# A two-layer convolution block: a new order of its second layer, and 64 channels expanded two phases at a time

## The chip, the cores and the metric

The kernel runs on one core of a Trainium2 chip. The core has a matrix engine (TensorE, PE in the profile; its weight loads are PEld), a vector engine (VectorE, DVE), an activation engine (ScalarE, ACT), GpSimd (POOL) and SyncE (SP), which here only issues DMAs. The metric is the device time of one execution in microseconds (us). The kernel before takes 4761.99 us, the median of three runs (4741.11 to 4764.95).

## The reference

Thirty-two images of 96 channels and 56 x 56 points pass through two layers. Cut to what matters:

```python
x = x + L0(group_norm(x))          # layer 0
x = x + L1(group_norm(x))          # layer 1

def L0(x):                         # inverted bottleneck, 4-bit weights and activations
    h = act_q(bn1(conv1x1(x, w1)))         # 96 -> 576 channels ("expand")
    h = act_q(bn2(depthwise3x3(h, w2)))    # 576 channels
    return x + bn3(conv1x1(h, w3))         # 576 -> 96 ("project")

def L1(x):                         # three groups of 32 channels
    x_0, x_05, x_1 = split(x)
    x_0  = conv3x3(x_0, conv0_w * gate(mean(x_0)))             # "spatial"
    F    = frft2d(x_05, alpha(mean(x_05)))                     # fractional Fourier transform
    F    = conv1x1(F, conv05_w * gate(mean(x_05)))             # "fractional mix"
    x_05 = abs(frft2d(F, -alpha)) / (H * W)                    # a square root at its end
    x_1  = irfft2(conv1x1(rfft2(x_1), conv1_w * gate(mean(x_1))))
    return conv3x3(concat(x_0, x_05, x_1), conv2_w)            # "final"
```

The group norms are over 32 groups of three channels, per image. The gates and `alpha` are small networks of the channel means.

## The kernel before

The program is a software pipeline over the images. While layer 0 of image i+1 is on its way, layer 1 of image i fills in. Both are given as lists of steps with weights, and `interleave` mixes two lists; a scheduler then fixes the order of every engine's instructions when the program is built. Each engine works through its own list in that order.

```python
    def layer0(i):
        xt = xts[i]
        def norm():                                     # statistics of the loaded image
            stats = p2.tile([C, NCH, 6], F32, tag="bn", name=f"bn{i}")
            for j in range(NCH):
                nc.vector.bn_stats(stats[:, j, :], xt[:, j * CN : (j + 1) * CN])
            mean, rstd, _ = group_stats(...)
        # ... split(k): DVE makes v, ACT rounds it to vh, DVE takes the rest vl; per quarter
        #     ("phase") of the image
        def expand(b, k):                               # block b of 128 channels, phase k
            ps = pair(f"pe{i}_{b}_{k}")
            for n, v in enumerate((s["vh"], s["vl"])):
                for h in range(2):
                    nc.tensor.matmul(ps[:, h, :HN], w1[:, 128 * b : 128 * (b + 1)],
                        v[:, k, HN * h : HN * (h + 1)], start=(n == 0), stop=(n == 1))
            src = q1s[turn["q1s"] % 3]
            quant_act(ps, A1[:, b : b + 1], B1[:, b : b + 1], src[:, :, :PH], ...)   # ACT to qt, DVE to q1s
            for g in range(blk(b) // G):                # four (last block: two) DMAs q1s -> qp
                nc.sync.dma_start(out=qps[(NB * i + b) % 3][...], in_=src[...])
        # ... depthwise(b, j): 8 matmuls into a pair `pd`, quant_act to qtd and q2
        # ... project(h, lo, hi): 72 matmuls into two pairs `pp`, then DVE adds them to x
```

PSUM is used as two pairs of banks (`pair`: pe, pd and pp share them) and four single banks (`bank`: all of layer 1). The image tiles `x` have three buffers, so the load of image i+2 goes to the buffer that image i-1 was stored from. `qt` has three buffers.

```python
        def mix_f(j):                                   # before: 4 steps, each both halves
            at = slice(HN * j, HN * (j + 1))
            for h in range(2):
                t = p2.tile([128, HN], F32, tag="zs", ...)
                nc.tensor.matmul(ps[:, :HN], g1[rows], s["xf"][rows, at], start=True, stop=True)
                # half 1 to zs on DVE, half 0 on ACT
                nc.sync.dma_start(out=s["z"][:, h, at], in_=t)          # to DRAM
            if j < 3: return
            # ... two DMAs z -> zh (the other way round in memory), eight DMAs z -> az
        # rows_f(g): matmuls pi of zh, copied to Y;  columns_f(g): matmuls pz of Y, plus az,
        # squared on ACT (sq), added on DVE (Z)
        def magnitude():
            for r in range(4):
                nc.scalar.activation(dst[:, :, r, :], s["Z"][G * r : G * (r + 1)], AF.Sqrt)   # to cat
        # spatial(h): ps -> cat;  hilbert(g): pr -> cat
        def final(j):                                   # rows 8j .. 8j+7 of the output
            for t in range(9):
                nc.tensor.matmul(ps[:C, :CN], wc[:, C * t : C * (t + 1)], cat[...], ...)      # pc
            nc.vector.scalar_tensor_tensor(part, ps[:C, :CN], bc, part, ALU.add, ALU.add)

        first = [(0.5, means), (1.0, gates), (0.1, norm)]
        steps = [(0.5, weights), (1.0, angles)] + each(1.1, mix_t, 4) + each(1.0, mix_f, 4)
        sp = each(2.7, spatial, 2)
        steps += sp[:1] + each(2.1, hilbert, 2) + each(1.3, rows_f, 4) + each(1.2, columns_f, 4)
        steps += [(0.0, magnitude)] + sp[1:]
        steps += each(6.7, final, NCH)
        return first, steps, [(0.0, store)]

    for i in range(B):
        conv, nxt = now["conv"], None
        if i + 1 < B:
            nxt = layer0(i + 1)
            conv[8:8] = nxt["norm"]
            at = 2 * (4 * NB - LEAD) + 1
            conv[at:at] = nxt["split"]
        interleave(conv, one[:-4])
        interleave(now["last"], one[-4:-2])             # project
        head, two, done = layer1(i)
        interleave(head + (nxt["first"] if nxt else []), one[-2:] + end)
        if i + 2 < B:
            load(i + 2)
        one, end, now = two, done, nxt
```

So layer 1 of an image gets five of its seven final convolutions under layer 0 of the next one, and two are held for the time in which the gates of the image after it are worked out.

Of the kernel before, what the change touches and what calls it, by code (L numbers as in the profile page):

```python
# [37 lines left out]
F32 = mybir.dt.float32  # L38
F32R = mybir.dt.float32r
# [3 lines left out]
AF = mybir.ActivationFunctionType  # L43
# [4 lines left out]
C, H, W = 96, 56, 56  # L48
HW = H * W
HID = 576  # L50
NB = 5
# [3 lines left out]
G = 32  # L55
NG0 = HID // G
PH = H // 2
PN = PH * PH
PW = PH + 2
PT = (PH + 1) * PW + 2  # L60
HN = PN // 2
HH = HW // 2
LOW = 64
LEAD = 7
L = 57
MAGIC = 1.5 * 2.0**23
TWO_PI = 6.283185
# [10 lines left out]
def blk(b):  # L78
    return 128 if b < NB - 1 else HID - 128 * (NB - 1)
# [7 lines left out]
def interleave(a, b):  # L87

    ta, tb = sum(c for c, _ in a) or 1, sum(c for c, _ in b) or 1
    i = j = 0  # L90
    ca = cb = 0.0
    while i < len(a) or j < len(b):
        if j >= len(b) or (i < len(a) and ca * tb <= cb * ta):
            ca += a[i][0]
            a[i][1]()
            i += 1
        else:
            cb += b[j][0]
            b[j][1]()
            j += 1  # L100
# [3 lines left out]
def block_kernel(ctx: ExitStack, tc: tile.TileContext, out: bass.AP, a: dict):  # L104
    nc = tc.nc
# [3 lines left out]
    cp = ctx.enter_context(tc.tile_pool(name="const", bufs=1))  # L109
    xp = ctx.enter_context(tc.tile_pool(name="xp", bufs=3))  # L110
    p1 = ctx.enter_context(tc.tile_pool(name="p1", bufs=1))
    p2 = ctx.enter_context(tc.tile_pool(name="p2", bufs=2))
    p3 = ctx.enter_context(tc.tile_pool(name="p3", bufs=3))
    dp = ctx.enter_context(tc.tile_pool(name="dp", bufs=2, space=bass.MemoryType.DRAM))
    ps0 = ctx.enter_context(tc.tile_pool(name="ps0", bufs=2, space=PSUM))
    ps1 = ctx.enter_context(tc.tile_pool(name="ps1", bufs=4, space=PSUM))

    def bank(pool, name):
        return pool.tile([128, 512], F32, tag="bank", name=name)

    def pair(name):

        return ps0.tile([128, 2, 512], F32, tag="pair", name=name)
# [19 lines left out]
    def prepare():  # L143
# [29 lines left out]

        w1f = load_tmp("w1")
        quantise(w1f, C, HID, "1")
        w1 = cp.tile([C, NB * 128], F32R, tag="w1r", name="w1r")
        nc.vector.memset(w1f[:, HID:], 0.0)
        nc.vector.tensor_copy(w1, w1f)
        w2 = load_tmp("w2")
        quantise(w2, 128, NG0 * 16, "2")  # L180
        mask = load_tmp("mask")
# [55 lines left out]
    w1, dw, w3, A1, B1, A2, B2, A3, B3, cw = prepare()  # L237
# [12 lines left out]


    q1s, qps = [], []
    for k in range(3):
        t = cp.tile([128, PH, PW], FP8, tag=f"q1s{k}", name=f"q1s{k}")
        nc.gpsimd.memset(t, 0.0)
        q1s.append(t)
    for k in range(3):
        t = cp.tile([128, 4, PT], FP8, tag=f"qp{k}", name=f"qp{k}")
# [10 lines left out]
    for k in range(2):  # L269
        t = cp.tile([G + 1, 1], F32, tag=f"hid{k}", name=f"hid{k}")  # L270
# [4 lines left out]
    g1 = cp.tile([128, 128], F32, tag="g1", name="g1")  # L275
# [9 lines left out]
    zh = cp.tile([LOW + W, G, LOW], F32, tag="zh", name="zh")  # L285
# [32 lines left out]
    turn = {"q1s": 0}  # L318
# [6 lines left out]
    def layer0(i):  # L325

        xt = xts[i]
        s = {}
# [37 lines left out]
            nc.vector.tensor_scalar(xt, xt, s["one"], s["off"], ALU.mult, ALU.add)  # L366

        def expand(b, k):
            ps = pair(f"pe{i}_{b}_{k}")
            for n, v in enumerate((s["vh"], s["vl"])):  # L370
                for h in range(2):
                    nc.tensor.matmul(  # L372
                        ps[:, h, :HN],
                        w1[:, 128 * b : 128 * (b + 1)],
                        v[:, k, HN * h : HN * (h + 1)],
                        start=(n == 0),
                        stop=(n == 1),
                    )
            src = q1s[turn["q1s"] % 3]
            turn["q1s"] += 1  # L380
            quant_act(ps, A1[:, b : b + 1], B1[:, b : b + 1], src[:, :, :PH], f"e{i}_{b}_{k}")

            n, at = blk(b) // G, PW * (k // 2) + k % 2
            for g in range(n):
                nc.sync.dma_start(  # L385
                    out=qps[(NB * i + b) % 3][G * k : G * (k + 1), g, at : at + PH * PW],
                    in_=src[g * G : (g + 1) * G].rearrange("c h w -> c (h w)"),
                )

        def depthwise(b, j):  # L390
            g = 4 * b + j
# [38 lines left out]
                nc.vector.bn_stats(stats2[i][:, j, :], xt[:, j * CN : (j + 1) * CN])  # L430


        ex = [(0.75, lambda b=b, k=k: expand(b, k)) for b in range(NB) for k in range(4)]
        de = [(1.45, lambda g=g: depthwise(g // 4, g % 4)) for g in range(NG0)]
        conv = []
        for g in range(NG0):
# [13 lines left out]
    def layer1(i):  # L450
        xt = xts[i]
        s = {}
# [191 lines left out]
        def mix_f(j):  # L644

            if j == 0:
                s["z"] = dp.tile([128, 2, HH], F32, tag="z", name=f"z{i}")
            at = slice(HN * j, HN * (j + 1))
            for h in range(2):
                t = p2.tile([128, HN], F32, tag="zs", name=f"zs{i}_{j}_{h}")  # L650
                rows = slice(LOW * h, LOW * h + G + 2)
                ps = bank(ps1, f"pm{i}_{j}_{h}")
                nc.tensor.matmul(ps[:, :HN], g1[rows], s["xf"][rows, at], start=True, stop=True)  # L653
                if h:
                    nc.vector.tensor_copy(t, ps[:, :HN])
                else:
                    nc.scalar.copy(t, ps[:, :HN])
                nc.sync.dma_start(out=s["z"][:, h, at], in_=t)
            if j < 3:
                return  # L660
            z = s["z"].rearrange("o u n -> o (u n)")
            for k in range(2):
                nc.sync.dma_start(
                    out=zh[LOW * k : LOW * k + W, :, :W], in_=z[G * k : G * (k + 1)].rearrange("o (h w) -> h o w", w=W)
                )
            az = p1.tile([128, H // 4, 2, W], F32, tag="az", name=f"az{i}")
            s["az"] = az
            for r in range(4):
                for t in range(2):
                    src = z[2 * G + G * t : 3 * G + G * t].rearrange("o (q r w) -> r o q w", r=4, w=W)  # L670
                    nc.sync.dma_start(out=az[G * r : G * (r + 1), :, t, :], in_=src[r])

        def rows_f(g):
# [20 lines left out]
        def columns_f(g):  # L694

            if g == 0:
                s["Z"] = p1.tile([128, H // 4, W], F32, tag="Z", name=f"Z{i}")
            n = 4 if g < 3 else 2
            ps = bank(ps1, f"pz{i}_{g}")
            for k in range(n):  # L700
                q = 4 * (4 * g + k)
                nc.tensor.matmul(
                    ps[:, 2 * W * k : 2 * W * (k + 1)],
                    Y[:, q : q + 4, :].rearrange("p h c -> p (h c)"),
                    cs,
                    start=True,
                    stop=True,
                )
            m = 2 * W * n
            sq = p2.tile([128, 8 * W], F32, tag="zs", name=f"sq{i}_{g}")  # L710
            add = s["az"][:, 4 * g : 4 * g + n].rearrange("p q t w -> p (q t w)")
            nc.vector.tensor_tensor(sq[:, :m], ps[:, :m], add, ALU.add)
            nc.scalar.activation(sq[:, :m], sq[:, :m], AF.Square)
            z = sq[:, :m].rearrange("p (q r w) -> p q r w", r=2, w=W)
            nc.vector.tensor_tensor(s["Z"][:, 4 * g : 4 * g + n, :], z[:, :, 0, :], z[:, :, 1, :], ALU.add)

        def magnitude():
            dst = cat[G : 2 * G, 1 : 1 + H, 1 : 1 + W].rearrange("p (q r) w -> p q r w", r=4)
            for r in range(4):
                nc.scalar.activation(dst[:, :, r, :], s["Z"][G * r : G * (r + 1)], AF.Sqrt)  # L720

        def spatial(h):

# [35 lines left out]
        def each(c, f, n):  # L759
            return [(c, lambda k=k: f(k)) for k in range(n)]  # L760

        first = [(0.5, means), (1.0, gates), (0.1, norm)]
        steps = [(0.5, weights), (1.0, angles)] + each(1.1, mix_t, 4) + each(1.0, mix_f, 4)
        sp = each(2.7, spatial, 2)
        steps += sp[:1] + each(2.1, hilbert, 2) + each(1.3, rows_f, 4) + each(1.2, columns_f, 4)
        steps += [(0.0, magnitude)] + sp[1:]
        steps += each(6.7, final, NCH)
        return first, steps, [(0.0, store)]

# [1 line left out]
    now = layer0(0)  # L771
# [3 lines left out]
    one, end = [], []  # L775
    for i in range(B):
        conv, nxt = now["conv"], None
        if i + 1 < B:
            nxt = layer0(i + 1)
            conv[8:8] = nxt["norm"]  # L780
            at = 2 * (4 * NB - LEAD) + 1
            conv[at:at] = nxt["split"]


        interleave(conv, one[:-4])
        interleave(now["last"], one[-4:-2])
        head, two, done = layer1(i)
        interleave(head + (nxt["first"] if nxt else []), one[-2:] + end)
        if i + 2 < B:
            load(i + 2)  # L790
        one, end, now = two, done, nxt
# [86 lines left out]
def _layout(inputs):  # L878
# [3 lines left out]
    f = np.float32  # L882
    k = _constants()
# [2 lines left out]

    def hidden(v):

        p = np.zeros((NB * 128,) + v.shape[1:], f)
        p[:HID] = v  # L890
        return np.moveaxis(p.reshape((NB, 128) + v.shape[1:]), 0, 1)

    k["x"] = np.asarray(inputs["x"])
# [79 lines left out]
```

## Time and profile before

| | before |
|---|---|
| time, median of 3 runs | 4761.99 us |
| profiled span | 4750.5 us |
| TensorE matmul busy | 4293.0 us, 90% |
| VectorE busy | 2393.3 us, 50% |
| ScalarE busy | 2177.6 us, 46% |
| DMA moved | 249.58 MB, 53 GB/s on average |
| longest matmul groups | pc (final) 1620.7, pd (depthwise) 956.8, pe (expand) 434.7 + 351.7 |

How to read the lines that follow. A group is written as output <- inputs by tile name, so `pm<-xf,g` is the matmul of the fractional mix and `zs<-pm` its copy out of PSUM. A line of waits names who waited, for whom, how long in total, how often and the longest. In the timeline each line has its start, its length, the engine, the line of the kernel, the operation, and in brackets how long the engine was idle before it and what ended that. A line of windows has the stretch, its length, and each engine's busy time (and number of instructions) in the order PE, PEld, DVE, ACT, POOL, then the granted share of TensorE's clock, the share of DMA time and GB/s. A wait that ends with several semaphores is put down to one of them.

Tile names: `bn` statistics of a loaded image, `x` image tile, `vv` and `xf` inputs of the fractional mix, `pm` its product, `z`, `zh`, `az` its way through DRAM, `pi` and `pz` the two transform steps, `cat` the input of the final convolution, `pc` its output, `pp` the projection, `pj`, `pvv`, `px`, `po`, `pmb` smaller matmuls of layer 1.

### The profile page before, as it was taken

The numbers are of one execution on the slowest core, as the hardware profiler recorded it, in microseconds if no ns is written. First come the engines' busy times: TensorE is split into PE (matmuls) and PEld (weight loads), VectorE is DVE, ScalarE is ACT, GpSimd is POOL, SyncE is SP. The second block draws the span as 40 slices with busy tenths as digits, with TensorE's granted clock in tenths as the row PEclk, the third lists the DMA queues.
The fourth block names the chain that finished last, engine by engine and source line by source line (L and its number), as shares of the span: only waits on it lengthen the run. The fifth ranks groups of instructions, "written<-read, shape, count | busy, mean of one in ns | idle before, by whom it ended". The sixth has DMA issues, their size and how long they took to land.

```text
span 4750.5 us, 59888 instructions
## 1 busy us (share of the span) xinstructions
PE 4293.0 (90%) x21632; PEld 2471.1 (52%) x21632; DVE 2393.3 (50%) x5385; ACT 2177.6 (46%) x2824; POOL 176.7 (4%) x209
## 2 busy tenths in 40 slices
PE   3799999999998999999999999999999999999987
PEld 2545555545555555555555555455555555555544
DVE  5545545545445455455454455454454554555532
ACT  3534445444455444455444454444454444554431
POOL 1000000000000000000000000000000000000000
PEclk9899999999999999999999999999999999999998
DMA  2212222211223211222211222122222112222112
GB/s 72 44 48 45 42 61 65 64 46 39 48 62 65 62 38 36 59 64 65 58 40 39 58 65 64 43 42 48 62 65 63 35 39 58 65 64 53 33 34 48
DMA packets 397243, 249.58 MB, mean 53 GB/s; under 512 B 283233, under 2 KB 390100, under 8 KB 390804
## 3 DMA queue, kind: packets, MB, share of 16 engines
q1 hardware_dynamic: 394368, 242.76, 23.0%
q8 instruction: 172, 2.82, 0.3%
q10 hardware_dynamic: 2580, 2.99, 0.2%
q14 instruction: 123, 1.01, 0.1%
HBM read 92.90 MB, written 89.92 MB: 38 GB/s over the span
## 4 chain that ended last, share of the span: by engine, by line
PE 63%; DVE 14%; DMA 11%; ACT 6%; issue 4%; SPq 3%; POOL 0%; DVEq 0%; ACTq 0%; POOLq 0%
PE pc L746 31%; PE pd L398 12%; PE pp L414 5%; DMA zh<-z 4%; PE pe L372 4%; PE pm L653 4%; DMA qp<-q1s 3%; PE pi L678 3%; ACT cat L720 2%; SPq L385 2%; DMA z<-zs 2%; DVE bn L333 2%; DVE q1s L315 2%; DVE x L426 2%; DMA x<-in_x_dram 1%
## 5 line engine op out<-in xcount | busy, mean ns | idle before, releaser
L746 PE MATMUL pc<-cat,wc 96*96 96x448 f32 x4032 | 1620.7, 557 | 60.9 <-ACT cat L720 60.9
L746 PEld LDWEIGHTS pc<-cat,wc 96*96 96x96 f32 x4032 | 664.1, 168 | 895.5 <-issue 809.0
L398 PE MATMUL pd<-qp,dw 128*128 128x392 fp8e4 x4608 | 956.8, 353 | 43.0 <-ACT qtd L313 37.9
L313 ACT ACTIVATE qtd<-pd,o,s 128x784 int16<-128x784 f32 x576 | 576.4, 1001 | 908.1 <-PE pd L398 878.2
L313 ACT ACTIVATE qte<-pe,o,s 128x784 int16<-128x784 f32 x640 | 635.9, 998 | 685.3 <-PE pe L372 669.5
L398 PEld LDWEIGHTS <-dw 128*128 128x128 fp8e4 x4608 | 447.4, 102 | 502.2 <-issue 203.9
L372 PE MATMUL pe<-vh,w1r 96*128 96x392 f32 x1280 | 434.7, 422 | 71.1 <-DVE x L426 41.2
L315 DVE TENSOR_SCALAR q1s<-qte 128x784 fp8e4<-128x784 int16 x640 | 358.8, 562 | 240.4 <-ACT qte L313 144.3
L315 DVE TENSOR_SCALAR q<-qtd 128x784 bf16<-128x784 int16 x576 | 207.0, 359 | 499.1 <-ACT qtd L313 496.4
L754 DVE SCALAR_TENSOR_TENSOR x<-pc,bc,x 96x448 f32<-96x448 f32 x224 | 152.0, 679 | 582.7 <-PE pc L746 581.2
L372 PE MATMUL pe<-vl,w1r 96*128 96x392 f32 x1280 | 351.7, 357 | 0.0
L372 PEld LDWEIGHTS pe<-vh,w1r 96*128 96x128 f32 x1280 | 221.8, 198 | 222.2 <-issue 94.9
L653 PE MATMUL pm<-xf,g 34*128 34x392 f32 x512 | 202.7, 768 | 107.5 <-DVE bn L333 105.0
L414 PE MATMUL pp<-q,w3q 32*96 32x392 bf16 x4608 | 255.8, 327 | 2.2 <-DVE x L426 2.2
L372 PEld LDWEIGHTS pe<-vl,w1r 96*128 96x128 f32 x1280 | 246.1, 198 | 0.5
L426 DVE SCALAR_TENSOR_TENSOR x<-pp,s,x 96x392 f32<-96x392 f32 x256 | 142.2, 616 | 175.8 <-PE pp L414 175.8
L414 PEld LDWEIGHTS <-w3q 32*96 32x96 bf16 x4608 | 182.0, 118 | 84.6 <-issue 31.5
L726 PE MATMUL ps<-xq,g 128*128 128x392 f32 x512 | 201.1, 536 | 0.0
L678 PE MATMUL pi<-cs,zh 120*120 120x112 f32 x1024 | 136.9, 295 | 63.8 <-DMA zh<-z 57.9
L333 DVE BATCH_NORM_STATS2 bn<-x 96x6 f32<-96x448 f32 x224 | 121.1, 608 | 133.6 <-DMA x<-in_x_dram 133.6
L361 ACT CAST vh<-v 96x392 fp32r<-96x392 f32 x256 | 126.2, 516 | 128.7 <-DVE v L353 127.9
L678 PEld LDWEIGHTS pi<-cs,zh 120*120 120x120 f32 x1024 | 131.6, 209 | 75.6 <-DVE cat L640 24.1
(149 smaller groups left out, 3881.5 us busy)
## 6 DMA issues: line engine op xcount, KB each, us to landing
qp<-q1s SPq DMA_DIRECT2D x2304, 26.2 KB
z<-zs SPq DMA_DIRECT2D x256, 196.0 KB
x<-in_x_dram SPq DMA_DIRECT2D x32, 1176.0 KB
out_dram<-x SPq DMA_DIRECT2D x32, 1176.0 KB
zh<-z SPq DMA_DIRECT2D x64, 392.0 KB
az<-z SPq DMA_DIRECT2D x256, 98.0 KB
xf<-vv SPq DMA_DIRECT2D x128, 6.1 KB
prep<-in_w_dram ACTq DMA_DIRECT2D x1, 864.0 KB
```

The costliest lines, as they stand in the source:

```text
L313: nc.scalar.activation(t.rearrange("p (h n) -> p h n", h=2), ps[:, :, :HN], AF.Relu, bias=offset, scale=scale)
L315: nc.vector.tensor_scalar(dst, src, 15.0, None, ALU.min, saturate=False if dst.dtype == FP8 else None)
L333: nc.vector.bn_stats(stats[:, j, :], xt[:, j * CN : (j + 1) * CN])
L372: nc.tensor.matmul(ps[:, h, :HN], w1[:, 128 * b : 128 * (b + 1)], v[:, k, HN * h : HN * (h + 1)], start=(n == 0), stop=(n == 1),)
L398: nc.tensor.matmul(ps[:, h, :HN], dw[:, g, t, :], view(qps[(NB * i + b) % 3][:, j, :], at, [[PW, PH // 2], [1, PH]]), start=(t == 0), stop ...
L414: nc.tensor.matmul(s["pp"][k // 2][:C, k % 2, :HN], w3[rows, g, :], s["q2"][rows, g, HN * h : HN * (h + 1)], start=(g == 0), stop=(g == NG ...
L426: nc.vector.scalar_tensor_tensor(part, src, A3, part, ALU.mult, ALU.add)
L653: nc.tensor.matmul(ps[:, :HN], g1[rows], s["xf"][rows, at], start=True, stop=True)
L678: nc.tensor.matmul(ps[: LOW + W, 2 * W * k : 2 * W * (k + 1)], zh[:, c : c + 2, :].rearrange("p c w -> p (c w)")[:, : LOW + W], cs, start= ...
L726: nc.tensor.matmul(ps[:, :HN], s["g0"][:, 128 * k : 128 * (k + 1)], view(xq, PH // 2 * h * (W + 2) + k, [[W + 2, PH // 2], [2, PH]]), star ...
L746: nc.tensor.matmul(ps[:C, :CN], wc[:, C * t : C * (t + 1)], cat[:, CR * j + dy : CR * j + dy + CR, dx : dx + W], start=(t == 0), stop=(t = ...
L754: nc.vector.scalar_tensor_tensor(part, ps[:C, :CN], bc, part, ALU.add, ALU.add)
```

## The change

Five things are changed together.

1. The statistics of the next image and the split come later in layer 0's list: `norm` six places ahead of `split`, where it stood at the eighth place. The angles come ahead of the weights.
2. The fractional mix is done half by half (all four pieces of the upper half of the image, then the lower half), and each half is read back to `zh` when it is written. The copies `zs` have four buffers. Both spatial steps come ahead of the transform.
3. The square roots are taken in two parts, the first after two of four column steps, so that the first final convolutions need only the first part.
4. Four final convolutions, not two, are held for the time of the next gates.
5. The last block of layer 0 has 64 of the 576 channels. Before, each of its four phases was a step with half of the 128 output rows unused. Now a step takes two phases: the weights are padded on either side, so that one phase lands in the lower 64 rows and the next in the upper 64. It has 8 matmuls and one eviction. There are five buffers `q1s` instead of three.

The aim is to take waits from TensorE's path and evictions from ScalarE and VectorE.

```diff
-    for k in range(3):
+    for k in range(NQ):                                # NQ = 5
         t = cp.tile([128, PH, PW], FP8, tag=f"q1s{k}", name=f"q1s{k}")
 ...
         def expand(b, k):
             ps = pair(f"pe{i}_{b}_{k}")
-            for n, v in enumerate((s["vh"], s["vl"])):
+            m = blk(b)
+            n = 128 // m
+            for e in range(2 * n):
                 for h in range(2):
+                    at = 128 * b + m * (n - 1) * (1 - e // 2)
                     nc.tensor.matmul(
                         ps[:, h, :HN],
-                        w1[:, 128 * b : 128 * (b + 1)],
-                        v[:, k, HN * h : HN * (h + 1)],
-                        start=(n == 0),
-                        stop=(n == 1),
+                        w1[:, at : at + 128],
+                        s["vl" if e % 2 else "vh"][:, k + e // 2, HN * h : HN * (h + 1)],
+                        start=(e == 0),
+                        stop=(e == 2 * n - 1),
                     )
 ...
         def mix_f(j):
-            at = slice(HN * j, HN * (j + 1))
-            for h in range(2):
-                t = p2.tile([128, HN], F32, tag="zs", name=f"zs{i}_{j}_{h}")
 ...
+            h, k = divmod(j, 4)
+            nc.tensor.matmul(ps[:, :HN], g1[rows], s["xf"][rows, HN * k : HN * (k + 1)], start=True, stop=True)
+            t = p4.tile([128, HN], F32, tag="zs", name=f"zs{i}_{j}")
 ...
+            if k < 3:
                 return
+            for t in range(2):
+                src = s["z"][G * t : G * (t + 1), HH * h : HH * (h + 1)].rearrange("o (h w) -> h o w", w=W)
+                nc.sync.dma_start(out=zh[LOW * t + PH * h : LOW * t + PH * (h + 1), :, :W], in_=src)
 ...
-        def magnitude():
+        def magnitude(h):
             dst = cat[G : 2 * G, 1 : 1 + H, 1 : 1 + W].rearrange("p (q r) w -> p q r w", r=4)
+            at = slice(8 * h, min(8 * h + 8, H // 4))
             for r in range(4):
-                nc.scalar.activation(dst[:, :, r, :], s["Z"][G * r : G * (r + 1)], AF.Sqrt)
+                nc.scalar.activation(dst[:, at, r, :], s["Z"][G * r : G * (r + 1), at], AF.Sqrt)
 ...
-        steps = [(0.5, weights), (1.0, angles)] + each(1.1, mix_t, 4) + each(1.0, mix_f, 4)
-        sp = each(2.7, spatial, 2)
-        steps += sp[:1] + each(2.1, hilbert, 2) + each(1.3, rows_f, 4) + each(1.2, columns_f, 4)
-        steps += [(0.0, magnitude)] + sp[1:]
+        steps = [(1.0, angles), (0.5, weights)] + each(1.1, mix_t, 4) + each(0.6, mix_f, 8)
+        sp, co = each(2.7, spatial, 2), each(1.2, columns_f, 4)
+        steps += sp + each(2.1, hilbert, 2) + each(1.3, rows_f, 4)
+        for h in range(2):
+            steps += co[2 * h : 2 * h + 2] + [(0.1, lambda h=h: magnitude(h))]
         steps += each(6.7, final, NCH)
 ...
-            conv[8:8] = nxt["norm"]
-            at = 2 * (4 * NB - LEAD) + 1
+            at = 2 * (4 * NB - 2 - LEAD)
             conv[at:at] = nxt["split"]
-        interleave(conv, one[:-4])
-        interleave(now["last"], one[-4:-2])
+            conv[at - 6 : at - 6] = nxt["norm"]
+        interleave(conv, one[: -HOLD - 2])             # HOLD = 4
+        interleave(now["last"], one[-HOLD - 2 : -HOLD])
         head, two, done = layer1(i)
-        interleave(head + (nxt["first"] if nxt else []), one[-2:] + end)
+        interleave(head + (nxt["first"] if nxt else []), one[-HOLD:] + end)
```

## The prediction

> **What bounds the kernel now.** I read the busy shares first, then the waits of TensorE, then one image in windows, then that image's timeline around its waits.
>
> ```profile
> PE 4293.0 (90%) x21632; PEld 2471.1 (52%) x21632; DVE 2393.3 (50%) x5385; ACT 2177.6 (46%) x2824; POOL 176.7 (4%) x209
> ...
> PE   3799999999998999999999999999999999999987
> ...
> PEclk9899999999999999999999999999999999999998
> ```
>
> TensorE (PE) is busy for 90%, more outside the first and last slices, and nothing else is over half. So only three things can move the time: PE's work, PE's waits, and the clock granted to it, which is never quite full. The windows of single images (cut from one `pj` matmul to the next) separate them; these are the two extremes of the clock and the mean of 27 images:
>
> ```profile
> 3923.32:4072.45 149.13, 138.85 (x677) 78.88 (x677) 74.00 (x166) 68.06 (x89) 4.81 (x6) 0.91 0.22 52
> 4072.45:4213.75 141.30, 129.59 (x677) 75.35 (x677) 73.82 (x166) 67.85 (x89) 4.81 (x6) 0.98 0.25 55
> ...
> sum 3891.74, PE 3595.24 PEld 2063.33 DVE 1996.03 ACT 1833.71 POOL 129.86; mean PE 133.16 PEld 76.42 DVE 73.93 ACT 67.92 POOL 4.81
> ```
>
> The same 677 matmuls took 138.85 us at clock 0.91 and 129.59 at 0.98. Clock time lost: 149.13 x 0.09 = 13.4 us and 141.30 x 0.02 = 2.8 us. So 9.3 us of busy time go with 10.6 us lost, 0.87 each, and at full clock the work is 129.59 - 0.87 x 2.8 = 127.1 us. A mean image of 3891.74 / 27 = 144.1 us is then 127.1 of work, 133.2 - 127.1 = 6.1 of slow clock, and 144.1 - 133.2 = 10.9 of waiting. Which waits:
>
> ```profile
> PE pm L653 <- DVE bn L333: 105.0, 29, 4.3
> PE pc L746 <- ACT cat L720: 60.9, 32, 6.7
> PE pi L678 <- DMA zh<-z: 57.9, 27, 5.0
> PE pe L372 <- DVE x L426: 41.2, 31, 1.3
> PE pd L398 <- ACT qtd L313: 37.9, 77, 4.9
> PE pmb L295 <- DVE mvb L293: 31.8, 31, 4.8
> ```
>
> Per image about 3.6, 1.7, 1.8, 1.3, 0.9 and 0.9 us. One image's timeline shows where the largest comes from:
>
> ```profile
> 2326.67 0.68 DVE L754 SCALAR_TENSOR_TENSOR x<-pc,bc,x 96x448 f32<-96x448 f32 x1
> 2327.38 0.35 SPq L757 DMA_DIRECT2D out_dram<-x  x1
> 2333.92 0.52 SPq L130 DMA_DIRECT2D x<-in_x_dram  x1
> 2342.19 3.78 DVE L333 BATCH_NORM_STATS2 bn<-x 96x6 f32<-96x448 f32 x7 [4.24 <-DMA x<-in_x_dram]
> 2342.23 3.26 SPq L603 DMA_DIRECT2D xf<-vv  x4
> 2346.04 2.43 PE L653 MATMUL pm<-xf,g 34*128 34x392 f32 x4 [3.63 <-DVE bn L333]
> ```
>
> The last final convolution of image i-1 is added at 2326.67; only then can it be stored; the load of image i+2 into the same buffer starts 6.54 us after the store, lands 8.27 us later, and its statistics take 3.78. VectorE (DVE) stands at those statistics for 4.24 us and everything queued behind them waits. The rows `xf<-vv` are also issued only when that load has landed, because the built program gives DMAs eight semaphores in turn and the eighth after the load must wait for it. So this wait has two causes that end together. The slow clock follows it:
>
> ```profile
> 2342.44:2346.04 3.60, 0.00 (x0) 0.03 (x1) 3.60 (x8) 1.19 (x2) 0.00 (x0) 1.00 0.03 5
> 2346.77:2363.84 17.07, 17.07 (x43) 7.79 (x43) 5.29 (x13) 5.95 (x8) 0.00 (x0) 0.50 0.31 104
> ```
>
> PE is empty for 3.60 us and then runs at half clock for 17.07.
>
> **What the Trainium skill says.** "TensorE: Matmul & The Clock Gate", Part 1 (the HAM clock gate): PE's clock is halved when a free-running window of about 3.4 us saw it idle, and is given back after a busy one. The trace agrees in kind: 17.07 us is five times 3.41; but it stayed halved through full work, longer than one window. The same page, on the array's sub-arrays and queue depths: ScalarE and VectorE are strict FIFO. The 4.24 us agree: evictions that were ready wait behind the statistics. "ScalarE: Activation LUTs", What ACT_TABLE_LOAD costs: 1283 ns for a load. The trace has 1283 in all three places. The changed program has still three loads per image, since Square needs none after Sqrt; splitting the roots adds no load.
>
> **The change part by part.** The order of each engine is known from the built program; times are those of the trace before.
>
> Last 64 channels. 5 x 4 steps become 4 x 4 + 2, each of the two with 8 matmuls in place of 4: the count on PE stays at 80 per image. Gone are two evictions: 2 x 1.00 us on ScalarE (ACT) and 2 x 0.56 on DVE, on engines at 46 and 50%. On the path: about 0, and some of the 0.9 of pd.
>
> Statistics later. Before, `bn` stood on DVE after the first PQ copy; now it stands after the fourth and after one more q1s, and ahead of `zs` 1 and 3. I walk it from the end of the last final convolution, t = 0. Its addition is no longer behind weights: it ends at 0.75 (before: about 2.9). Store at 0.85, load at 0.85 + 6.54 = 7.4 (say 7.5), landed at 15.8, statistics done at 19.6. Then q2 0.36, q1s 0.56, zs1 0.57: 21.2. On PE stand pj, pe, pd, pvv, px 0 to 3, two more pe and pd, one pe, pm 0 to 3, pd, pe, pm 4 and 5: 0.7 + 0.8 + 1.5 + 3.5 + 0.8 + 1.35 + 0.45 + 0.8 + 1.4 + 0.85 + 1.8 + 1.4 + 0.85 + 0.85 = 17.05. pm 6 needs the PSUM bank that zs1 frees, so it waits 21.2 - 17.05 = 4.2 us. The `xf` rows now come before the eighth DMA and are in time. So one of the two causes goes and the other stays: 3.6 becomes 4.2, a loss of 0.6.
>
> Four held convolutions. Behind po now stand two more finals (2 x 6.9 us) before pj. The weights and angles need about 9 us: pj's 0.4 to 0.6 goes and the pd waits of 0.4 to 0.5 there too. Gain: about 1.0.
>
> Mix by halves, and both spatial parts moved up. From pm 6 to pi stand pm 2 x 0.43, two pd and two pe, ps 5.8, pr 3.6, two more of each: about 19 us of PE work (more at half clock) against z writes, two half reads of `zh` and the copies between, some 15 us. Gain: the 1.8 of pi.
>
> Roots in two parts. Between pz and pc stand now two pd instead of ps, pd and pe: 3.4 + 2 x 1.3 = 6.0 us against 8.3 before. On ACT the first roots come after an eviction, five casts `vh` and two squares. From the start of pz: qte to 1.1, vh to 2.1, sq to 2.7, second sq (behind DVE's vl, sq, vl) 4.1, three vh as DVE makes v to 6.4, table 7.7, four roots of 448 elements at about 0.58 (a square of 448 takes 0.58) to 10.0. Before, the roots also ended 10.0 after pz began (2382.16 to 2392.15). So halving them gives nothing, since the casts of the next image now stand ahead, and the filler is gone: 1.7 becomes 4.0. Loss: 2.3.
>
> Projection. Before, a final convolution (7.01 us) stood between its two halves; now they follow each other. The second half needs the PSUM pair that DVE empties: 1.3 us as at pe after pp. And it begins with 44 matmuls of one pair alone: the first half did so and took 4.72 where the second took 3.19; I take 1.3. Loss: 2.6, half of it as PE work.
>
> Sum per image at equal clock: 0.6 - 1.0 - 1.8 + 2.3 + 2.6 = +2.7, and -0.4 for the other pd waits: +2.3. Waiting becomes about 12, work 128.4.
>
> Clock. One wait long enough to empty a window stays (4.2), a second (4.0) appears; the 1.3 + 1.3 + 0.9 around the projection lie in 13 us. I estimate 8.5 us of slow clock in place of 6.1 (range 6 to 12): +2.4.
>
> Together +4.7 per image, x 30 = 141; start and end give back about 8 (evictions of the first image, four held finals under the last gates). 4762 + 133 = 4895 us.
>
> **The rivals.** First: the statistics no longer stop PE, as intended. If the load lands before DVE reaches them, 4.2 and most of the slow clock go, and the image is about 136: 4520 us. For it speaks only the later place; against it, that load's chain is 19.6 us long and PE has 17 us of work.
> Second: everything as walked but the clock no worse: +2.3 x 30 - 8, 4823 us.
> Third: each of the two long waits brings a half-clock stretch of 17 us as the one shown: 0.87 x 17 = 15 us instead of 6.1, +11 per image, 5090 us.
> Fourth: DMAs of half size crowd the one issuing queue and pi waits again, +2 per image: 4955 us.
>
> **Range and chances.** The walk is good to 1 us per image at each of its steps, some 60 us in all; the clock to 3 us per image. Predicted 4895, eight times in ten 4780 to 5000. Over 2% slower begins at 4857: 0.60; within 2%: 0.28; over 2% faster (below 4667) needs the first rival: 0.12.
>
> **What will show it.** In the waits of PE: pm (sixth and later) still behind `bn` or `zs` at about 4 us; pc behind the roots at 4 where 1.7 was; a new pp wait behind x at 1.3; pi behind `zh` gone; pj gone. In the windows: clock below 0.947 on average. The prediction is wrong if pm no longer waits, or if the clock rises above 0.96.

## The result, and the profile after

| | before | after |
|---|---|---|
| time, median of 4 runs each, us | 4760.41 (4741.11 to 4764.95) | 4903.57 (4893.83 to 4908.27) |
| ratio, 95% interval | | 1.031 [1.027, 1.034] |
| profiled span, us | 4750.5 | 4898.6 |
| mean granted clock of TensorE | 0.941 | 0.911 |

The change makes the kernel 3.1% slower. The first view of the page after:

```profile
PE 4482.3 (92%) x21632; PEld 2633.1 (54%) x21632; DVE 2369.5 (48%) x5322; ACT 2146.9 (44%) x2888; POOL 177.9 (4%) x211
...
PEclk9899989989898999899898989998998989999998
```

VectorE (DVE) and ScalarE (ACT) have less to do, as intended: 24 and 31 us less. TensorE (PE) has the same 21632 matmuls and is busy for 189 us more. The window of one image after, and the sums over 27 images (stretch, length, then busy time of PE, PEld, DVE, ACT and POOL, clock, DMA share, GB/s):

```profile
2409.27:2559.90 150.63, 140.47 (x677) 82.22 (x676) 73.27 (x164) 67.05 (x90) 4.81 (x6) 0.91 0.20 51
...
sum 4044.57, PE 3773.31 PEld 2216.62 DVE 1976.80 ACT 1806.90 POOL 129.85; mean PE 139.75 PEld 82.10 DVE 73.21 ACT 66.92 POOL 4.81
```

An image takes 4044.57 / 27 = 149.8 us, 5.7 more than before, and PE works 139.75 of it, 6.6 more. So PE waits less than before: 10.0 us in place of 11.0. The half-clock stretches of the clock's records add up to 26.6 us per image in place of 15.6. Which matmuls became longer is read from the groups of the page (the first number behind the bar is the busy time in us):

```profile
L756 PE MATMUL pc<-cat,wc 96*96 96x448 f32 x4032 | 1738.9, 591 | 109.9 <-ACT cat L730 109.9
...
L661 PE MATMUL pm<-xf,g 34*128 34x392 f32 x512 | 238.2, 621 | 106.8 <-DMA qp<-q1s 50.2
...
L424 PE MATMUL pp<-q,w3q 32*96 32x392 bf16 x4608 | 291.7, 327 | 35.4 <-DVE x L436 35.4
```

Before, the final convolutions pc took 1620.7 us, the mix pm 202.7 and the projection pp 255.8. Per image (difference over 32) that is +3.7, +1.1 and +1.1; the two expand groups pe add 1.2, and the other groups give some of it back. The number of matmuls in each group is unchanged. The waits of PE after:

```profile
PE pc L756 <- ACT cat L730: 109.9, 32, 4.6
PE pm L661 <- DMA qp<-q1s: 50.2, 14, 4.1
...
PE pp L424 <- DVE x L436: 35.4, 32, 1.1
PE pm L661 <- DMA xf<-vv: 31.8, 10, 4.3
...
PE pm L661 <- issue: 24.8, 7, 3.7
```

Two large waits are left: 3.4 us of pc behind the roots, and 3.3 us of pm in sum of its three lines (one wait with several semaphores, put down now to one and now to another). The wait of pi is gone, that of pp is new. The same stretch as was shown of before, around the wait of pm:

```profile
2409.38 0.68 DVE L764 SCALAR_TENSOR_TENSOR x<-pc,bc,x 96x448 f32<-96x448 f32 x1 [6.09 <-PE pc L756]
...
2415.63 0.83 SPq L613 DMA_DIRECT2D xf<-vv  x1
2416.58 0.45 SPq L133 DMA_DIRECT2D x<-in_x_dram  x1
2417.09 2.40 SPq L613 DMA_DIRECT2D xf<-vv  x3
2424.30 3.78 DVE L338 BATCH_NORM_STATS2 bn<-x 96x6 f32<-96x448 f32 x7 [3.40 <-DMA x<-in_x_dram]
...
2424.46 3.78 PE L661 MATMUL pm<-xf,g 34*128 34x392 f32 x8 [3.02 <-DMA qp<-q1s]
```

PE stops at the first mix, not at the seventh. The rows xf are issued around the load of the image, and the mix starts when that load has landed. From 2426.27 on PE's clock is halved for 17.1 us. And the mix itself is slow: the windows of its two groups, counting instructions of that line alone (PE and PEld busy, clock):

```profile
2424.40:2428.30 3.90, 3.78 (x8) 1.61 (x8) 0.74 0.25 77
2432.20:2437.80 5.60, 5.59 (x8) 2.50 (x8) 0.50 0.33 84
```

### The profile page after: what moved, and what is told of

Same layout as the page of the kernel before. It is cut to its first block, busy times and chain, and to the rows that moved or that the text cites. A ratio compares the mean times of both kernels' runs of the same rounds, so it can differ in the third digit from the quotient of the medians.

```text
span 4898.6 us, 59704 instructions
## 1 busy us (share of the span) xinstructions
PE 4482.3 (92%) x21632; PEld 2633.1 (54%) x21632; DVE 2369.5 (48%) x5322; ACT 2146.9 (44%) x2888; POOL 177.9 (4%) x211
## 4 chain that ended last, share of the span: by engine, by line
PE 83%; DVE 7%; ACT 4%; DMA 3%; issue 2%; SPq 1%; DVEq 0%; ACTq 0%; POOL 0%
PE pc L756 35%; PE pd L408 16%; PE pe L381 8%; PE pp L424 6%; PE pm L661 5%; PE ps L736 4%; DVE x L436 2%; PE pi L687 2%; PE px L626 2%; DMA xf<-vv 1%; ACT cat L730 1%; DVE bn L440 1%; DMA qp<-q1s 1%; PE pr L644 1%; PE pr L641 1%
## 5 line engine op out<-in xcount | busy, mean ns | idle before, releaser
L756 PE MATMUL pc<-cat,wc 96*96 96x448 f32 x4032 | 1738.9, 591 | 109.9 <-ACT cat L730 109.9
L756 PEld LDWEIGHTS pc<-cat,wc 96*96 96x96 f32 x4032 | 710.8, 179 | 1024.8 <-issue 898.6
L318 ACT ACTIVATE qte<-pe,o,s 128x784 int16<-128x784 f32 x576 | 574.0, 1002 | 810.9 <-PE pe L381 792.7
L320 DVE TENSOR_SCALAR q1s<-qte 128x784 fp8e4<-128x784 int16 x576 | 321.8, 563 | 257.3 <-ACT qte L318 213.5
L661 PE MATMUL pm<-xf,g 34*128 34x392 f32 x512 | 238.2, 621 | 106.8 <-DMA qp<-q1s 50.2
L424 PE MATMUL pp<-q,w3q 32*96 32x392 bf16 x4608 | 291.7, 327 | 35.4 <-DVE x L436 35.4
L424 PEld LDWEIGHTS <-w3q 32*96 32x96 bf16 x4608 | 206.2, 117 | 120.2 <-DVE x L436 47.2
L661 PEld LDWEIGHTS pm<-xf,g 34*128 34x128 f32 x512 | 108.3, 222 | 198.8 <-issue 150.6
L748 DVE TENSOR_SCALAR cat<-ps,b 32x392 f32<-32x392 f32 x128 | 79.9, 624 | 142.4 <-ACT cat L750 142.4
L736 PEld LDWEIGHTS ps<-xq,g 128*128 128x128 f32 x512 | 104.0, 204 | 80.4 <-issue 79.3
```

The costliest lines, as they stand in the source:

```text
L318: nc.scalar.activation(t.rearrange("p (h n) -> p h n", h=2), ps[:, :, :HN], AF.Relu, bias=offset, scale=scale)
L320: nc.vector.tensor_scalar(dst, src, 15.0, None, ALU.min, saturate=False if dst.dtype == FP8 else None)
L424: nc.tensor.matmul(s["pp"][k // 2][:C, k % 2, :HN], w3[rows, g, :], s["q2"][rows, g, HN * h : HN * (h + 1)], start=(g == 0), stop=(g == NG ...
L661: nc.tensor.matmul(ps[:, :HN], g1[rows], s["xf"][rows, HN * k : HN * (k + 1)], start=True, stop=True)
L736: nc.tensor.matmul(ps[:, :HN], s["g0"][:, 128 * k : 128 * (k + 1)], view(xq, PH // 2 * h * (W + 2) + k, [[W + 2, PH // 2], [2, PH]]), star ...
```

## The experiments

Each row is one kernel. The ratio is to the kernel before on the same chip; the kernel before took 4753.8 to 4763.9 us on the chips used. Image, idle, half clock and busy are means of 27 images of the one profiled execution, which in e7 and e10 is the shortest of its runs (us; idle and busy of PE from its records, half clock from the clock's).

| run | what differs | time, us | ratio, 95% interval | image | idle | half clock | busy |
|---|---|---|---|---|---|---|---|
| before | | 4760.4 | | 144.1 | 11.0 | 15.6 | 133.2 |
| after | all five parts | 4903.6 | 1.031 [1.027, 1.034] | 149.8 | 10.0 | 26.6 | 139.8 |
| e1 | after, mix alternated | 4730.2 | 0.994 [0.992, 0.996] | 144.0 | 10.0 | 20.2 | 134.0 |
| e2 | after, two finals held | 4956.7 | 1.043 [1.040, 1.046] | 151.6 | 10.1 | 32.6 | 141.5 |
| e3 | after, casts behind the roots | 4686.1 | 0.985 [0.983, 0.987] | 142.7 | 6.9 | 19.3 | 135.8 |
| e4 | before, 64-channel step alone | 4908.5 | 1.033 [1.030, 1.035] | 150.1 | 15.2 | 22.0 | 134.8 |
| e5 | e4, casts behind the roots | 4688.3 | 0.985 [0.982, 0.988] | 142.7 | 9.4 | 17.6 | 133.3 |
| e6 | e1 and e3 together | 4522.3 | 0.949 [0.945, 0.953] | 137.7 | 6.6 | 14.8 | 131.1 |
| e7 | after, xf on another queue | 4785.3 | 1.006 [1.005, 1.008] | 145.6 | 8.2 | 21.4 | 137.4 |
| e8 | after, roots in one part | 5034.0 | 1.057 [1.054, 1.060] | 154.0 | 15.2 | 29.6 | 138.8 |
| e9 | e6 and e7 together | 4526.5 | 0.951 [0.948, 0.954] | 138.1 | 5.9 | 15.8 | 132.1 |
| e10 | e6, statistics early again | 4599.9 | 0.967 [0.961, 0.972] | 139.3 | 7.6 | 13.7 | 131.7 |
| e11 | e6, spatial branch split again | 4496.5 | 0.945 [0.941, 0.948] | 137.0 | 5.7 | 14.0 | 131.3 |
| e12 | e11, image load behind xf | 4526.5 | 0.949 [0.944, 0.954] | 137.7 | 5.0 | 11.5 | 132.6 |

**e1: the order of the mix.** The change does four mixes of the upper half (rows 0 to 33 of the array) and then four of the lower (rows 64 to 97); before, each step did one of each.

```diff
-        steps = ... + each(0.6, mix_f, 8)
+        steps = ... + [(0.6, lambda j=j: mix_f(j)) for j in (0, 4, 1, 5, 2, 6, 3, 7)]
```

> The changed kernel with one edit: the eight matmuls of the fractional mix stand as 0 4 1 5 2 6 3 7 (upper and lower half in turn) instead of 0 to 7; every other instruction of TensorE keeps its place. Theory: by halves, four matmuls in a row use the same 34 rows of the array, and each weight load waits for the matmul before it (0.33 us a piece at full clock in the changed kernel, 0.65 at half); in turn they use two row groups and take 0.23 and 0.42 as before. Then pm goes from 238 us busy to about 200 and the kernel from 4904 to 4800-4850. Rival: pm is slow only because the clock is; then pm stays near 238 and the time at 4904.

It gained more than that: 4730.2 us, less than before. Everything else stands in the same place on PE. The windows of the mix in this run, as above:

```profile
2341.10:2343.00 1.90, 1.68 (x8) 1.04 (x8) 1.00 0.13 33
2346.60:2348.30 1.70, 1.59 (x8) 0.69 (x8) 1.00 0.71 240
```

Eight matmuls take 1.6 us at full clock. In the kernel after they follow each other 329 ns apart at full clock (in single records), which would be 2.6 us, and 653 ns apart at half clock, the 5.59 us of its second window. In the second window of this run the single records show two matmuls of different rows that start 6 or 7 ns apart, and the next two 329 ns after the first two: they run at the same time. I had thought only of weight loads that lie bare; the gain is the matmul itself. "TensorE: Matmul & The Clock Gate", Part 3 (packing small matmuls), The mechanism, of the Trainium skill says just this: matmuls in different row groups of the array overlap, with starts some 4 ns apart. The trace agrees. The group pm falls from 238.2 to 126.8 us over the kernel, 3.5 per image; with the shorter work 6.3 us of half clock go too.

**e2: two held finals instead of four.** Meant to put a final convolution between the two halves of the projection again.

```diff
-HOLD = 4
+HOLD = 2
```

> The changed kernel with two final convolutions held instead of four. One of them stands again between the two halves of the projection. Theory: the wait of pp behind x (1.1 us per image) and the slow start of the second half (4.4 us instead of 3.2) go, and the slow clock behind the projection shrinks; the waits of pj and pd (about 1.3 per image) come back. 4780 to 4875 us. Rival: the held finals are what the change gains by, and without them it is slower: above 4920.

Slower, by 53 us, but it isn't the test it was meant to be: the built order puts the final ahead of both halves, so they still follow each other. Its timeline:

```profile
2550.51 3.20 PE L424 MATMUL pp<-q,w3q 32*96 32x392 bf16 x72
2554.95 4.39 PE L424 MATMUL pp<-q,w3q 32*96 32x392 bf16 x72 [1.24 <-DVE x L436]
```

What follows is only that in this order holding four finals helps: pj waits 0.4 us per image again and pd 0.95 in place of 0.33. These are the smaller part of the loss: pc even waits 1.1 us less, and the mix is busy for 321.9 us in place of 238.2, 2.6 per image more, with 6.0 us more of half clock in an image.

**e3: the casts behind the roots.** The splitting of the next image's input (`split`, eight casts vh on ACT) stands four places later, at entry 26 of layer 0's list (the statistics not counted); the statistics stay. The change had moved it from 26, its place in the kernel before, to 22: in the list it had come earlier, not later as said under The change.

```diff
-            at = 2 * (4 * NB - 2 - LEAD)
+            at = 2 * (4 * NB - 2 - LEAD) + 4
             conv[at:at] = nxt["split"]
-            conv[at - 6 : at - 6] = nxt["norm"]
+            conv[at - 10 : at - 10] = nxt["norm"]
```

> The changed kernel with the split of the next image four places later in layer 0's list (statistics unmoved). ScalarE then makes all eight casts vh after the roots instead of five of them before. Theory: the wait of pc behind the roots (3.45 us per image) is made by those casts and falls to about 0.8; with the clock that follows it the kernel goes to 4780-4830. Rival: the roots wait for the chain of squares anyway; pc still waits over 3 us and the time stays at 4904.

It took 217 us off. The wait of pc behind the roots goes from 109.9 to 34.1 us in the whole kernel. But not all of this is the casts, since PE's order changes too. The start of pz and the first pc of an image, in the kernel after:

```profile
2467.66 2.16 PE L711 MATMUL pz<-cs,Y 120*128 120x112 f32 x18
...
2477.11 13.21 PE L756 MATMUL pc<-cat,wc 96*96 96x448 f32 x30 [3.44 <-ACT cat L730]
```

and in e3:

```profile
2503.57 2.16 PE L711 MATMUL pz<-cs,Y 120*128 120x112 f32 x18
...
2511.95 7.76 PE L756 MATMUL pc<-cat,wc 96*96 96x448 f32 x20 [0.98 <-ACT cat L730]
```

From one to the other it is 9.45 us and 8.38, so the roots come 1.1 us earlier. PE works 6.0 us of it in the kernel after and 7.4 in e3, where a third depthwise step stands ahead of pc. Of the 2.5 us less wait, 1.1 belong to the casts and 1.4 to that step. A piece of a final also lies between the projection's halves here, and the wait of pp falls from 1.1 to 0.2 us. The group pc goes from 1738.9 to 1650.2 us of busy time. That its slow clock comes with its wait is not shown: in e8 the wait is 8.6 us per image and pc is busy for 1718.6 us.

**e4 and e5: the 64-channel step alone.** e4 is the kernel before with that part of the change only; e5 has its casts four places later as well (`... + 5`).

```diff
-            at = 2 * (4 * NB - LEAD) + 1
+            at = 2 * (4 * NB - 2 - LEAD) + 1
```

> The kernel before with the 64-channel step alone (three q1s buffers). Theory: the two evictions fewer on ScalarE and VectorE gain nothing on TensorE's path, but with two steps fewer in the list the casts vh of the next image now stand ahead of the roots, so pc waits about 3 us instead of 1.7: 4780 to 4820 us. Rival: the lighter engines show on the path: 4700 to 4740.

> The kernel before with the step of the last 64 channels alone, as in the run of that part alone (4908.5 us, 150.1 us for an image, 6.69 us of wait for the attention's first matmul), but with the splitting of the next image's input put four places later in the list of work, so that its eight casts stand behind the roots again. Theory: the loss of that part was only the place of the casts in ScalarE's order. The wait pc<-cat goes back to 1.7 or less, the image to 143 to 145, and the time to 4700 to 4780. Rival: the single step itself is dear (eight matmuls for two phases behind one buffer pair, six copies of one source): then the wait pi<-zh or pe stays up and the time stays above 4850.

The part that I had put at nothing on the path costs, alone, as much as the whole change: 4908.5 us. ACT in e4 (start, length, operation; five more casts lie in the part left out, two ahead of it):

```profile
2465.68 0.57 ACT L720 ACTIVATE sq<-sq 128x448 f32<-128x448 f32 x1
...
2473.82 0.52 ACT L364 CAST vh<-v 96x392 fp32r<-96x392 f32 x1
2474.35 1.28 ACT L727 ACT_TABLE_LOAD   x1
2475.65 3.51 ACT L727 ACTIVATE cat<-Z 32x784 f32<-32x784 f32 x4
```

and in e5:

```profile
2356.04 0.58 ACT L720 ACTIVATE sq<-sq 128x448 f32<-128x448 f32 x1 [0.47 <-DVE sq L719]
...
2360.64 3.50 ACT L727 ACTIVATE cat<-Z 32x784 f32<-32x784 f32 x4
2381.67 0.93 ACT L364 CAST vh<-v 96x392 fp32r<-96x392 f32 x2
```

The edit counts the place of the split from the number of expand steps. Two steps fewer put it at entry 22 in place of 26, and all eight casts come ahead of the roots; e5 puts it at 26 again. From the first square to the last root it is 13.5 us in e4 and 8.1 in e5. The wait of pc is 6.7 and 1.0 us per image, behind the same matmuls of PE (8.9 us from pz to pc in both). So here, with the roots in one part, the place of the split is the whole loss; the step itself, with the split at its old place, makes the kernel 1.5% faster than before.

**e6: both edits.**

> The kernel after with both edits that helped: the row groups of the mix alternated (alone: 4730.2, an image of 144.0 us) and the casts behind the roots (alone: 4686.1, 142.7 us). Theory of separate causes: the two gains add (173 and 217 us): some 4510, and an image of 136 to 137 us (40 windows of the clock of 3.413 us), with the pm piece at 200 us in sum and pc<-cat at 1.0. Rival: both gains came through the same half clock, and the second finds little left of it: 4620 to 4686, an image of 140 or more. Both agree that the mix's busy time falls back to about 200 us; they differ in the sum.

4522.3 us: the gains add, 381 us of the 391 of their sum. The rival, that both live on the same half clock, falls. The mix is busy for 132.0 us, not the 200 that both had said.

**e7, e9 and e12: why the rows xf are late.** e7 issues the four copies of xf from the GpSimd queue, e9 does it in e6, and e12 leaves the queue but issues the load of the image later.

```diff
-                    nc.sync.dma_start(out=s["xf"]...
+                    nc.gpsimd.dma_start(out=s["xf"]...
```

> The kernel after, with the three copies of xf issued from the GpSimd queue instead of the SP queue, where they stand behind the 1.18 MB load of the image. Theory: they land late (at 2424.1 us in the image read) because of the load; on another queue they land some 3 us after their issue, the wait of 3.0 us before the first mix goes, and what is left is a wait of 1 us or less at the sixth mix behind bn and the eviction zs1. The image loses 2 to 3.4 us: 4790 to 4850. Rival: the load keeps the 16 engines themselves busy, so the copies land no sooner on any queue: the wait of 3 us stays and the time stays within 4890 to 4920.

> The kernel with both edits that helped (4522.3 us, 6.6 us idle in an image) and also the copies of xf on the GpSimd queue, which alone took 118 us from the kernel after. Theory: the wait of 3.4 us ahead of the mix shrinks to 1.5 or less here too, and with it one clock window of half speed: an image of 133 to 134 us and 4400 to 4460. Rival: the shorter mix now stands right behind the seven bn_stats, so the wait moves to zs<-pm and stays at 3: 4500 to 4540.

e7 gained 118 us, but not for the reason given. Its timeline:

```profile
2357.90 2.24 POOL L613 DMA_DIRECT2D xf<-vv  x4 [37.02 <-DVE vv L609]
2358.92 0.52 SPq L133 DMA_DIRECT2D x<-in_x_dram  x1
...
2365.03 2.87 PE L661 MATMUL pm<-xf,g 34*128 34x392 f32 x8 [0.99 <-DMA xf<-vv]
...
2366.82 3.78 DVE L338 BATCH_NORM_STATS2 bn<-x 96x6 f32<-96x448 f32 x7 [3.31 <-DMA x<-in_x_dram]
```

The completion of each copy is read from its semaphore. The two issued before the load were there 1.1 and 1.2 us after the end of their issue; the two issued after it, 5.4 and 6.9 us after, although they are 6 KB each and on another queue. So it isn't the queue that holds them, but the load on the same DMA engines. What e7 gained is the earlier issue: the third copy starts 0.1 us behind the load, not 1.4, and lands 1.9 us ahead of it, where in the kernel after it landed together with it (2424.32 and 2424.28). The first mix waits for this copy. In "DMA: Bandwidth & Descriptors", Queues, rings and completion order, the Trainium skill says that a completion's increment is written only after all earlier writes of that DMA engine, also of its other queues. That can be a part of the delay at most: by the DMA packet records of e7 the data of the third copy moved only at 2362.3 to 2363.0, 2.8 us after the end of its issue, and that of the fourth at 2364.8 to 2365.6, 4.6 us after it. The increments were complete 1.9 and 1.4 us after the data. In e9 the alternated mix needs all the rows sooner, and the gain is gone: 0.7 us less idle but 1.0 us more of half clock, the same time as e6 within the intervals. The rival's range held, though the wait (2.9 us in a steady image) is mostly for xf and not for zs.

e12 tests it the direct way, in the fastest kernel: the load goes into the list of work (sketch of the edit).

```diff
-        if i + 2 < B:
-            load(i + 2)
+            conv[8:8] = [(0.0, lambda k=i + 1: load_now(k))]   # the tile is taken as before
```

> The fastest kernel so far (both edits and the spatial branch split again: 4496.5 us, 5.6 us idle in an image) with the load of the next image but one issued later: behind the four copies of xf and most of the writes of z, so that the seven bn_stats stand on VectorE behind the last eviction zs. Theory: the copies were late because the load was issued among them (in the two runs with the other queue, copies issued up to 1.1 us after the load still landed 5.4 to 6.9 us later, those issued before it 1.2 us later). Issued ahead of the load, all four land about 1.2 us after their issue: the wait ahead of the mix falls from 3.6 to 1.7 or less, no bn stands ahead of zs, and the image comes to 131 to 134 us: 4320 to 4420. Rival: the wait only moves: the last two writes of z and the reads of zh now stand behind the load, and pi (or pma behind the late statistics) waits 2 us or more; the time stays within 4450 to 4530.

The mechanism holds and the time doesn't follow. From the waits of e12:

```profile
PE pe L384 <- ACT qte L321: 61.3, 28, 11.2
...
PE pi L690 <- DMA zh<-z: 18.0, 20, 2.6
...
PE pm L664 <- DMA xf<-vv: 8.5, 19, 2.6
```

The mix starts 1.3 us after the issue of the third copy ends, and its waits fall from 3.6 us in a steady image (three lines in e11) to 0.4. In their place come 1.5 us of pe behind evictions and 0.5 of pi behind zh, which now stands behind the load; and the new order separates some pairs of the mix (pm 138.8 to 167.4 us). The rival's range held, though pi waits 0.8 us in all and not 2.

**e8: the roots in one part.**

```diff
-            at = slice(8 * h, min(8 * h + 8, H // 4))
-            for r in range(4):
+            at = slice(0, H // 4)
+            for r in range(4) if h else ():
```

> The kernel after with the roots in one part behind all four columns (four roots of 784 elements instead of eight of 448 and 336), all else as it was; three more casts and two squares then stand ahead of the first root. Theory of the prediction: two parts let the first attention piece start a root and more earlier; in one part the wait pc<-cat rises from 3.45 to between 5 and 7 and the time to 4940 to 5020. Rival: with the casts ahead the roots are late anyway and four fixed costs of a root are saved: the wait stays at 3 to 4 and the time within 4880 to 4920.

5034.0 us; the wait of pc more than doubles, beyond what I expected:

```profile
PE pc L756 <- ACT cat L730: 261.0, 32, 8.6
```

The work of PE from pz to pc is the same (6.0 us), and pc starts 14.6 us after pz in place of 9.5. So halving the roots brings the first part 5.2 us earlier.

**e10 and e11: two parts undone in e6.**

```diff
-            conv[at - 10 : at - 10] = nxt["norm"]
+            conv[8:8] = nxt["norm"]
```

> The kernel with both edits that helped (4522.3 us) but with the statistics of the next image where they stood before the change (ninth place of the list). The order of the engines shows that bn stays ahead of zs1 either way, and that only the chain behind it (aggregate, the two small matmuls pma and pva, the affine numbers) moves ahead of the last two mixes. Theory of the prediction: moving the statistics is worth next to nothing on the path: 4500 to 4560, the pm waits 3 to 4 in sum. Rival: the small matmuls then wait for the late bn in the middle of the mix, and the move is what saved 2 us or more: pma and pva show 1 to 2 us of wait and the time is 4580 to 4640.

```diff
-        steps += sp + each(2.1, hilbert, 2) + ...
+        steps += sp[:1] + each(2.1, hilbert, 2) + ...
+        # and sp[1:] behind the last roots
```

> The kernel with both edits that helped (4522.3 us) but with the spatial branch where it stood before the change: one half right behind the mix, one half at the end. Theory: the mix by halves alone doesn't bring zh in time; the eight spatial matmuls ahead of pi are the filler, so the wait pi<-zh returns with 1 to 1.8 us and the time goes to 4560 to 4620. Rival: the halves alone are enough; pi stays at 0 to 0.3 and the second spatial half at the end fills the wait for the roots: 4490 to 4530.

e10 lies in the range of the rival, at 4599.9. But pma and pva don't wait, so the rival's reason is wrong; the order changes elsewhere too: the pieces of the mix and of the finals come apart otherwise, and pp waits 1.1 us again. That the later statistics are worth 78 us by themselves isn't shown; on pm they change nothing (3.5 us either way). e11 is the fastest of all: pi waits 3.4 us in the whole kernel for zh, so the spatial step isn't needed ahead of pi, and the second one fills the wait for the roots (pc behind cat 0.8 us in the whole kernel). The order by halves isn't needed either: e6 and e11 take the halves in turn, and the first read of zh is issued 1.8 us behind the last write of z. What is left is the reading: pi starts 5.6 us after the issue of the last read in e11 and hardly waits, before it started 7.8 us after it and waited 1.8. Whether the half size of the reads does this, or what else the DMA engines have to do then, these runs don't separate.

## Why the prediction came out

The time predicted was 4895, and 4903.6 came. The direction was right, and so was the largest wait added, that of pc. That the total is so near is in part luck: under the sum lie errors of opposite sign.

Its sum, with its own rate of 0.87 us lost per us of clock time (half of 26.6, and of 15.6): waits 11.0 to 10.0, predicted about 12; clock loss 6.8 to 11.6, predicted 6.1 to 8.5; work 126.4 to 128.2, predicted 127.1 to 128.4. So waits came out 2 us too high and the clock 3 too low. Start and end gave back more than the 8 us: 30 x 5.66 = 170, measured 143.

- Last 64 channels, "about 0" on the path: wrong as a part by itself. The step gains 1.4 us per image (e5), and the place of the split that comes with it costs 7.4 where the roots are in one part (e4 against e5). I had the casts ahead of the roots in the step of the roots, and did not see that they belong to this part and can be put back.
- Statistics later, "the xf rows ... are in time", pm 6 waits 4.2 us: the size of the wait was near (3.6), its place and cause wrong. The copies are issued early, as I said, but the first mix waits for them, since they land with the load (e7, e12); pm 6 behind zs and bn doesn't wait.
- Four held finals, gain 1.0: right. pj's wait goes, pd's falls from 0.88 to 0.33; together 0.9.
- Mix by halves, gain 1.8: right in size. My reason, 19 us of work against 15, asked for more than is needed: e11 has neither the order by halves nor the spatial step ahead, and pi hardly waits. What the step missed is the row groups: the mix by halves gives up the matmuls that run side by side, 3.5 us per image and the slow clock with it (e1). This is the largest thing the prediction did not see.
- Roots in two parts, loss 2.3: right. PE's work from pz to pc went from 8.3 to 6.0 us, as said, and pc starts 9.5 us after pz where 10.0 was said, so the wait is 3.4 and not 4.0. "Halving them gives nothing" holds only for the sum of two effects: the casts ahead cost 5.7 us where the roots are in one part (e4 against e5), and the halving gives 5.2 back (e8).
- Projection, 1.3 of wait and 1.3 of slower work: right, 1.1 and 1.2 (its second half takes 4.39 us in place of 3.19).
- Clock, +2.4: too small by half; it is +4.8. Of this 2.7 go with the order of the mix (6.3 us of half clock, e1). The first rival, 4520 us because the statistics no longer stop PE, falls: the statistics don't stop it any more, but the rows xf do.

Removing two of the faults (e6) turns 3.1% slower into 5% faster, so the change as meant was good; its order was not.

## What to carry to other kernels

Where the place of one piece of work in a list is counted from the number of others, removing steps moves it: compare each engine's order and not only the diff, and ask which small operation of the next image now stands ahead of the one on the path. Keep short matmuls of different row groups next to each other. Issue small copies that something waits for ahead of a large load, and expect a wait removed near others to show up only in part (e9 and e12 gained nothing).

## What was not expected of the hardware

- Two matmuls of 34 rows each, at rows 0 and 64, cost the time of one: 329 ns per pair, 329 ns for one alone.
- Images of some of these kernels settle on multiples of the clock's window. After: 24 of 27 images take 149.8 to 150.8 us and three 146.7 to 146.8; 44 and 43 times 3.413 us are 150.2 and 146.8. That may be why a saving of wait pays nothing (e9) or more than itself (e1: 3.5 us of mix, 5.8 of image); it is argued from the lengths only. In the kernel before they don't settle: its 27 images spread from 140.6 to 149.1 us.
- A stretch at half clock can last several windows of full work: in the image shown 17.1 us (five windows) behind a wait of 3.0. That is rare in the kernel after, where 91 of 124 stretches last one or two windows and 3 last five or more; before, 7 of 72 did. What ends a stretch isn't settled by these runs.
